# A second cross-attention's weights added up on VectorE alone, with side work split and moved by steps

## The chip, the cores and the metric

The kernel runs on one core of a Trainium2 chip, in float32 throughout. The time is the device time of one execution in microseconds (us); of several executions the median is taken.

## The reference, cut to what matters

Four layers are added to x one after another. The arrays are x [4, 512, 256] and the context ctx [4, 1601, 256].

```python
x = x + L0_xattn(ctx, layernorm(x))   # 8 heads of 128; keys and values of [ctx; latents]
x = x + L0_ffn(layernorm(x))          # 8 experts, top 2, each with a capacity; h = gelu(xb @ w1); y = h @ w2
x = x + L1_xattn(ctx, layernorm(x))   # 8 heads of 32
x = x + L1_ffn(layernorm(x))          # 8 experts, top 2, no capacity

def L1_xattn(key, query):             # key = value = ctx, 1601 rows; query has 512
    q, k, v = split_heads(query @ Wq.T), split_heads(key @ Wk.T), split_heads(key @ Wv.T)
    attn = softmax(einsum('bhnd,bhmd->bhnm', q, k) * 32 ** -0.5)
    return einsum('bhnm,bhmd->bhnd', attn, v)      # heads joined again
```

## The kernel before, in words

The program has four stages in a row, one for each layer.

**First attention.** It takes the four batches one after another, and beside the last ones it already routes rows to the experts of the next stage (`route`: `normalize`, `choose`, `send`). `send` scatters the rows `xn` of a batch into the array `slot_x` in DRAM, with eight indirect transfers on GpSimd's queue (L312).

**First FFN** (`all_experts`). Each of the 8 experts has 512 places, taken in two halves. For each expert `fetched` loads the rows `sx` from `slot_x` and two weight matrices through SyncE's queue; `turned` transposes the rows on TensorE, `hidden` does the first matrix (ps_h) and the GELU, and `results` the second (ps_y). A generator `beside` is advanced between these pieces. In half 0 it is `keys_first`, which routes and sends the last batch and projects keys and values of batch 0 (`keys_values`); in half 1 it is `keys_next`, which projects those of batch 1, gathers and adds the first FFN's results of batch 0 (`collect`, `add_collected`), makes its queries and the first maxima. Another generator, `clears`, is advanced four times an expert: it writes zeros into the second half of `slot_y` and then fills `rows_a` and `rows_b`, the arrays in DRAM into which the second FFN's rows will be scattered, with 41 transfers. Between the halves the program loads a register and branches on it (L1286), in case an expert has too many rows. The instructions of this stage are ordered by a scheduler, apart from the places with a manual order.

**Second attention.** Its 16 units are (batch b, head group o of four heads, half f of the 512 queries). A unit has 13 tiles j of 128 keys, the last with 65 rows. For each tile `weights` computes scores in transposed form: keys on partitions, four heads times 256 queries on the free axis, by four matmuls into one PSUM tile ps_w. The left operand `keyed` holds the keys of a head group and a row of ones, the right one `asked` the queries and, at rows 32 and 96, the negated maximum of each query, so that the exponential on ScalarE needs no further shift. That exponential gives `pT`. `weigh` multiplies it with the values, accumulating over the tiles in ps_o. `add_weights` adds the `pT` of all tiles element by element, into `sum0` on VectorE and `sum1` on GpSimd:

```python
by_pool = (1, 4, 7, 10)
...
(nc.gpsimd if k else nc.vector).tensor_tensor(to, to, pT[:r], ALU.add)
```

Tiles 0 and 1 are written straight into the two sums; so VectorE adds 8 tiles of a unit and GpSimd 3. `closing` reduces the sums over the partitions by matmuls with ones (ps_n), transposes (tp_o), divides, and adds to x. It runs in three pieces, two steps apart.

The maxima of a unit are computed a unit ahead: `maxima` has TensorE form the scores once more with queries on partitions (ps_s, 7 pieces a unit) and VectorE reduce each of them (`tops`, L1124), `negated` reduces over the pieces into `shift`, and `to_row` turns `shift` into the rows of `asked`, by four transposes (ps_r, L1146) and two copies on ScalarE (L1150). ps_w, ps_s and all side work share a PSUM pool of three tiles.

In this stage the four computing engines follow the order in which the program is written (`in_order`). The loop takes two tiles a step, 104 steps and a few to finish; a step number counts tiles. In each step come the `weights` of two tiles, a piece of `maxima`, then for the two tiles of the step before the adds, then `weigh`, and last what `put` has placed at this step: `negated`, `to_row`, the gathers of `collect`, `queries` of the next batch, `keys_values` of the batch after, and `route2` of the batch before, which is the routing of the second FFN and ends in the scatters of its rows (L539). Transfers on SyncE's queue keep no such order, but are issued one after another.

**Second FFN.** It works on tiles of 128 scattered rows, whose number per expert is a matter of the routing; `route2` of the last batch runs at its start, beside tiles that the other batches have already filled.

## Time and profile before

| | |
|---|---|
| median of three executions | 2905.28 us (2904.32 to 2910.24) |
| the profiled execution, its own time | 2910.62 us |
| its span on the core | 2908.8 us |
| its mean granted TensorE clock | 0.972 |
| first attention | 0 to 1575 us of the span |
| first FFN | 1575 to 1943 us |
| second attention | 1943 to 2617 us |
| second FFN | 2617 to 2909 us |

The profile names engines PE (TensorE's matmuls), PEld (its weight loads), DVE (VectorE), ACT (ScalarE), POOL (GpSimd) and SP (SyncE); a q behind the name marks the engine's queue of transfers. A group's line gives the line of the kernel, engine, operation, output and inputs, their shapes and the number of instructions, then busy us and mean ns of one, then the idle time ahead of them with what ended most of it. A line of the timeline gives start, duration, and the same names, with the idle time ahead in brackets. A line of waits gives what waited, for whom, the total us, how often and the longest. The stage borders above are read from the first matmul of each stage. A granted clock of 1.00 is full speed.

### The profile page before, as it was taken

The page shows a single profiled execution, that of the slowest core. Times are in us where ns is not written, and L with a number is a line of the kernel's source. Part 1 is how long each engine was busy: PE and PEld are TensorE (multiplying, and loading weights), DVE is VectorE, ACT ScalarE, POOL GpSimd, SP SyncE. Part 2 cuts the span into 40 slices and gives each one's busy share as a digit, 9 for nine tenths or more (in the row PEclk, how much of TensorE's full clock was granted, in tenths as well). Part 3 has the DMA queues.
Part 4 walks back from the last instruction along what each step waited for, and adds up shares of the span by engine and source line. Part 5 has one row for each costly group of instructions (what it writes and reads, how often), then busy time and mean ns, then how long its engine had stood idle before and what let it go on. Part 6 is the DMA issues. An engine that isn't in the chain of part 4 may idle for free. (4 is left out here: it accounts for less than half of the span.)

```text
span 2908.8 us, 36010 instructions
## 1 busy us (share of the span) xinstructions
PE 2746.4 (94%) x13614; PEld 1860.1 (64%) x13614; DVE 1460.5 (50%) x2339; ACT 935.3 (32%) x1325; POOL 379.8 (13%) x290
## 2 busy tenths in 40 slices
PE   6999999999999999999998799998989989799998
PEld 2666666766766667666666577864444454458887
DVE  6445556554476444554454302148876767763111
ACT  3323334332343223332332111124434434352221
POOL 0000000100001000000000101002223414152442
PEclk9999999999999999999999999999999999899999
DMA  5444343434344333333335698820001011106563
GB/s 164 111 113 114 97 110 92 109 93 99 89 111 107 97 89 93 97 92 102 95 97 150 197 241 238 236 72 23 23 12 61 24 38 35 39 31 223 161 214 99
DMA packets 196435, 311.96 MB, mean 107 GB/s; under 512 B 43319, under 2 KB 117368, under 8 KB 193560
## 3 DMA queue, kind: packets, MB, share of 16 engines
q1 hardware_dynamic: 157512, 227.52, 29.4%
q0 software_dynamic: 14160, 46.31, 5.4%
q10 hardware_dynamic: 24576, 35.68, 4.8%
q8 instruction: 112, 1.84, 0.3%
q14 instruction: 75, 0.61, 0.1%
HBM read 111.73 MB, written 51.34 MB: 56 GB/s over the span
## 5 line engine op out<-in xcount | busy, mean ns | idle before, releaser
L810 DVE TENSOR_REDUCE top<-ps_s 128x1 f32<-128x2113 f32 x128 | 301.8, 2358 | 581.7 <-PE ps_s L802 581.7
L839 PE MATMUL ps_o<-pT,v 128*128 128x256 f32 x2176 | 521.7, 381 | 0.5 <-DVE inv L817 0.5
L802 PE MATMUL ps_s<-kT,qT 128*128 128x512 f32 (+1 forms) x1280 | 489.0, 526 | 6.0 <-ACT attn L816 6.0
L839 PEld LDWEIGHTS ps_o<-pT,v 128*128 128x128 f32 x2176 | 410.0, 191 | 115.1 <-issue 68.4
L816 ACT ACTIVATE attn<-ps_s,top 128x2113 f32<-128x2113 f32 x128 | 259.0, 2024 | 476.4 <-DVE top L810 446.1
L802 PEld LDWEIGHTS ps_s<-kT,qT 128*128 128x128 f32 x1280 | 241.4, 190 | 252.8 <-issue 236.7
L831 DVE STREAM_TRANSPOSE pT<-swapped 128x2176 f32<-128x2176 f32 x128 | 312.4, 2441 | 33.6 <-DMA swapped<-attn 23.3
L1124 DVE TENSOR_REDUCE tops<-ps_s 128x2 f32<-128x1024 f32 (+1 forms) x224 | 238.0, 1105 | 152.0 <-PE ps_s L1113 151.6
L1387 PE MATMUL ps_w<-asked,keyed 64*128 64x256 f32 (+1 forms) x1664 | 247.4, 420 | 20.3 <-DVE tops L1124 9.5
L751 PE MATMUL ps_k<-kvin,wkv 128*128 128x512 f32 (+1 forms) x640 | 262.7, 533 | 3.3 <-DVE mv_g L689 1.7
L785 PE MATMUL ps_v<-wkv,kvin 128*128 128x256 f32 x1088 | 254.5, 381 | 1.4 <-ACT v L792 1.4
L1387 PEld LDWEIGHTS ps_w<-asked,keyed 64*128 64x128 f32 (+1 forms) x1664 | 149.0, 192 | 147.0 <-ACT pT L1400 61.6
L1400 ACT ACTIVATE pT<-ps_w 128x1024 f32<-128x1024 f32 (+1 forms) x176 | 179.5, 1024 | 195.2 <-PE ps_w L1387 191.8
L785 PEld LDWEIGHTS ps_v<-wkv,kvin 128*128 128x128 f32 x1088 | 204.8, 190 | 36.6 <-ACT v L792 5.9
L1409 DVE TENSOR_TENSOR sum<-sum,pT 128x1024 f32<-128x1024 f32 (+1 forms) x128 | 183.0, 1430 | 10.3 <-ACT pT L1400 4.0
L764 ACT ACTIVATE kT<-ps_k,bqk 128x512 f32<-128x512 f32 (+1 forms) x160 | 96.9, 620 | 266.1 <-PE ps_k L751 123.4
L1409 POOL TENSOR_TENSOR sum<-sum,pT 128x1024 f32<-128x1024 f32 x48 | 122.5, 2553 | 350.3 <-ACT pT L1400 350.1
L751 PEld LDWEIGHTS ps_k<-kvin,wkv 128*128 128x128 f32 x640 | 115.9, 191 | 77.3 <-issue 66.7
L1113 PE MATMUL ps_s<-kv,qT 32*128 32x512 f32 (+1 forms) x1024 | 135.9, 579 | 14.7 <-ACT kv L1017 6.5
L792 ACT COPY v<-ps_v 128x512 f32<-128x512 f32 x144 | 79.9, 561 | 216.7 <-PE ps_v L785 142.1
L1197 PE MATMUL ps_h<-sxT,w 128*128 128x256 f32 x512 | 118.6, 390 | 4.8 <-ACT hT L1204 4.1
L1211 PE MATMUL ps_y<-w,hT 128*128 128x256 f32 x512 | 114.5, 380 | 0.3 <-DVE y L1219 0.2
(300 smaller groups left out, 2662.8 us busy)
## 6 DMA issues: line engine op xcount, KB each, us to landing
swapped<-attn SPq DMA_DIRECT2D x1536, 68.0 KB, 2.0
swapped<-attn ACTq DMA_DIRECT2D x512, 68.0 KB, 2.2
w<-in_w_dram SPq DMA_DIRECT2D x32, 1024.0 KB, 6.2
rows_b<-empty SPq DMA_DIRECT2D x36, 530.0 KB, 14.3
w_e<-in_wall_dram SPq DMA_DIRECT2D x5, 2052.0 KB
cw<-in_ctxT_dram SPq DMA_DIRECT2D x4, 1601.0 KB, 6.4
keyed<-kv SPq DMA_DIRECT2D x32, 200.1 KB, 3.6
ctx_b<-in_ctx_dram SPq DMA_DIRECT2D x3, 1536.0 KB
```

What stands on the lines that cost most here:

```text
L751: nc.tensor.matmul(ps[:, :n], lhsT=wkv[:, c, hs], rhs=kvin[:, c, : NB - 1, k, :] if k < 4 else kvin[:, c, NB - 1, :, :], start=c == 0, sto ...
L785: nc.tensor.matmul(ps[:, k, :], lhsT=flat_kvin[c][:, j * P : (j + 1) * P], rhs=wkv[:, c, cols], start=c == 0, stop=c == DC - 1,)
L802: nc.tensor.matmul(flat[:, j0 : j0 + n], lhsT=qT[:, t * P : (t + 1) * P], rhs=kT[:, j0 : j0 + n], start=True, stop=True,)
L810: nc.vector.tensor_reduce(top, flat[:, :L], AX.X, ALU.max, negate=True)
L816: nc.scalar.activation(attn[:, :L], flat[:, :L], AF.Exp, bias=top, accum_out=total)
L831: nc.vector.transpose(pT[:, :, k * P : (k + 1) * P].rearrange("p c (a i) -> p a c i", a=4), swapped.rearrange("p a (c i) -> p a c i", i=32),)
L839: nc.tensor.matmul(ps, lhsT=v[:, j - parts[part][0], (h % 2) * DH0 : (h % 2 + 1) * DH0], rhs=pT[:, j, :], start=j == 0, stop=j == NB - 1,)
L1113: nc.tensor.matmul(pss[i // 2][:, i % 2, at : at + n], lhsT=qTs[b][rows, o, q0 : q0 + P], rhs=kvs[b][0][o][rows, j0 : j0 + n], start=True, ...
L1124: nc.vector.tensor_reduce(tops[u][:, t : t + at // n, 2 * pair : 2 * pair + 2, j0 // 512], of, AX.X, ALU.max,)
L1387: nc.tensor.matmul(ps[:r, s, pair * QH : (pair + 1) * QH], lhsT=keyed[o][64 * s : 64 * s + 64, pair, j * P : j * P + r], rhs=asked[u % 3][ ...
L1400: nc.scalar.activation(pT[:r], ps[:r], AF.Exp)
L1409: (nc.gpsimd if k else nc.vector).tensor_tensor(to, to, pT[:r], ALU.add)
```

## The change

- `add_weights` works on VectorE only: tile 0 starts the sum, tiles 1 to 11 are added to it, and the last tile, of 65 rows, is not added, but summed over its own rows by `closing`'s matmuls. `sum1` is gone, and the pool of `pT` has 8 tiles where it had 6.
- `shift` has a quarter of its size. `negated` is one reduction, `to_row` one transpose and four activations on ScalarE, which scale by a column of `in_row` to leave zero in the rows that are not meant. Both come earlier: at 7 and 5 tiles ahead of the unit, where it was 5 and 4.
- The pieces of `closing` come one step earlier. `weigh` is issued ahead of the adds, and where the last tile of a unit and the first of the next are weighed in one step, the first of the next is put off to the following step (`late`).
- `route2` and `queries` yield more often, and lists of steps (`beside`, `bare`) place the pieces: a consumer is put a step or more after its producer. The counts (`counted`) are copied out of PSUM, the copy of `wbT` goes to ScalarE, and scatters go two to a yield. The gathers of `collect` come some 28 tiles earlier, and their zeros are written by GpSimd; `add_collected` comes four tiles earlier.
- In the first FFN `send` of the last batch moves to the end of half 0. The 41 fills of `rows_a` and `rows_b` move to the second attention, one for each tile from step 2 on. The first `keyed` tile is prepared at the end of half 0, the second at step 4 of the second attention and loaded at step 8. Three pieces of the maxima of unit 1 and `to_row` of unit 0 move into half 1, and `beside` is advanced three times an expert.

The diff, cut to its core (the added yields and some moved copies are left out):

```diff
--- before.py
+++ after.py
...
@@ -327,7 +331,7 @@
...
             g = gat.tile([P, D], F32, tag="g", name="g")
-            nc.vector.memset(g, 0.0)
+            nc.gpsimd.memset(g, 0.0)
             nc.gpsimd.indirect_dma_start(
...
@@ -489,11 +510,18 @@
...
         )
-        if b == B - 2:
-            nc.vector.tensor_copy(taken_a, taken2)
+        counted = two.tile([P, n, E], F32, tag="counted", name="counted")
+        nc.vector.tensor_copy(counted, ps)
+        tp = psum.tile([P, 4, P], F32, tag=tag, name="tp_w")
+        for t in range(n):
+            nc.tensor.transpose(tp[:E, t, :], wb[:, t, :], ident)
+        wbT = two.tile([E, n * P], F32, tag="wbT", name="wbT")
+        nc.scalar.copy(wbT, tp[:E, :n].rearrange("p i q -> p (i q)"))
+        yield
         for k in range(2):
             off, place, at, out_of = small("off2"), wide("place"), small("at2"), small("out_of")
-            nc.vector.tensor_tensor(place, hot[k], ps, ALU.mult)
+            nc.vector.tensor_tensor(place, hot[k], counted, ALU.mult)
             nc.vector.tensor_reduce(off, place, AX.X, ALU.add)
...
@@ -512,13 +540,25 @@
...
                 nc.vector.memset(place_a[k][:, mine_b], int(NOWHERE))
-        yield
-        tp = psum.tile([P, 4, P], F32, tag=tag, name="tp_w")
-        for t in range(n):
-            nc.tensor.transpose(tp[:E, t, :], wb[:, t, :], ident)
-        wbT = two.tile([E, n * P], F32, tag="wbT", name="wbT")
-        nc.vector.tensor_copy(wbT, tp[:E, :n].rearrange("p i q -> p (i q)"))
+            yield
+        def scatters():
...
+        sending = scatters()
         for t0 in range(0, n, 2):
...
@@ -1049,19 +1085,50 @@
...
     asked = [soon.tile([P, 2, QH], F32, name=f"asked{i}") for i in range(3)]
-    shift = [soon.tile([P, 2, 2, P], F32, name=f"shift{i}") for i in range(2)]
+    shift = [soon.tile([P, P], F32, name=f"shift{i}") for i in range(2)]
     for t in shift + asked:
...
+    keyed = [soon.tile([P, 2, M], F32, name="keyed0")]
+    def load_keys(b, o):
+        for pair in range(2):
+            for s in range(2):
+                i = 2 * pair + s
+                nc.sync.dma_start(
+                    keyed[o][64 * s : 64 * s + 32, pair, :],
+                    kvs[b][0][o][i * DH1 : (i + 1) * DH1, :],
+                )
+    def init_keys(t):
+        of_ones = ones[:, 0:1].to_broadcast([P, M])
+        nc.scalar.activation(t[:, 0], of_ones, AF.Copy, scale=in_row[:, 0:1])
+        nc.vector.tensor_scalar(t[:, 1], of_ones, in_row[:, 1:2], None, ALU.mult)
+    empty = soon.tile([P, PAY], F32, name="empty")
+    nc.gpsimd.memset(empty, 0.0)
+    nc.gpsimd.memset(empty[:, D : D + 1], NOWHERE)
...
         xn = soon.tile([P, NT, D], F32, tag="xn", name="xn")
-        mv = ln_moments(turns, x[b], NT)
-        root = ln_root(turns, mv, NT)
+        mv = ln_moments(turns, x[b], NT, some=())
+        for i in range(NT):
+            ln_moments(turns, x[b], NT, mv=mv, some=(i,))
+            if i + 1 < NT:
+                yield
+        ve = ln_variance(turns, mv, NT)
+        yield
+        root = ln_root(turns, mv, NT, ve)
         yield
...
             ln_apply(xn, x[b], mv, rs, i)
-        yield
+            if i in (0, NT - 1):
+                yield
         xnT = soon.tile([P, DC, S], F32, tag="xnT", name="xnT")
...
@@ -1129,25 +1197,26 @@
...
     def negated(u):
-        for pair in range(2):
-            nc.vector.tensor_reduce(
-                shift[u % 2][:, :, pair, 32::64],
-                tops[u][:, :, 2 * pair : 2 * pair + 2, :],
-                AX.X,
-                ALU.max,
-                negate=True,
-            )
+        nc.vector.tensor_reduce(
+            shift[u % 2].rearrange("q (s c) -> q s c", s=2)[:, :, 32:36],
+            tops[u].rearrange("q t (p s) n -> q s (t p) n", s=2),
+            AX.X,
+            ALU.max,
+            negate=True,
+        )
         tops.pop(u)
     def to_row(u):
-        ps = banks["m"].tile([P, 2, QH], F32, tag="m", name="ps_r")
-        for pair in range(2):
+        ps = banks["m"].tile([P, P], F32, tag="m", name="ps_r")
+        nc.tensor.transpose(ps, shift[u % 2], ident)
+        for r in (32, 96):
             for t in range(2):
-                nc.tensor.transpose(
-                    ps[:, pair, t * P : (t + 1) * P], shift[u % 2][:, t, pair, :], ident
-                )
-        for r in (32, 96):
-            nc.scalar.copy(asked[u % 3][r : r + 1], ps[r : r + 1])
+                nc.scalar.activation(
+                    asked[u % 3][r : r + 4, :, t * P : (t + 1) * P],
+                    ps[r : r + 4].unsqueeze(1).to_broadcast([4, 2, P]),
+                    AF.Copy,
+                    scale=in_row[r : r + 4, 2 + t : 3 + t],
+                )
...
@@ -1237,36 +1307,32 @@
...
-        empty = rt.tile([P, PAY], F32, name="empty")
-        nc.gpsimd.memset(empty, 0.0)
-        nc.gpsimd.memset(empty[:, D : D + 1], NOWHERE)
-        def clears():
...
-        clear = clears()
-        kvs = []
+        def clear_results(e):
+            tc.keep_in_program_order(
+                nc.sync.dma_start(
+                    slots(slot_y, e, 1), empty[:, :D].unsqueeze(1).to_broadcast([P, CT, D])
+                )
+            )
...
             choose()
-            send()
             yield
...
             kvs.append(kv)
-            for k, f in enumerate(steps):
+            for f in steps:
                 f()
-                if k % 2:
-                    yield
+                yield
+            for _ in range(len(steps) + 2, 3 * E - 4):
+                yield
+            send()
+            init_keys(keyed[0])
+            yield
+            load_keys(0, 0)
...
@@ -1311,10 +1375,13 @@
...
             negated(0)
-            to_row(0)
+            for g in range(3):
+                maxima(1, g)
+                yield
+                if g == 0:
+                    to_row(0)
         all_experts(1, keys_next())
-        assert next(clear, None) is None
...
@@ -1350,31 +1417,15 @@
...
         two = st.enter_context(tc.tile_pool(name="c_two", bufs=2))
-        six = st.enter_context(tc.tile_pool(name="c_six", bufs=6))
+        some = st.enter_context(tc.tile_pool(name="c_some", bufs=8))
         ps_s = st.enter_context(tc.tile_pool(name="c_ps_s", bufs=3, space=PSUM))
...
-        keyed = [one.tile([P, 2, M], F32, name=f"keyed{o}") for o in range(DC)]
-        of_ones = ones[:, 0:1].to_broadcast([P, M])
-        for t in keyed:
-            nc.scalar.activation(t[:, 0], of_ones, AF.Copy, scale=in_row[:, 0:1])
-            nc.vector.tensor_scalar(t[:, 1], of_ones, in_row[:, 0:1], None, ALU.mult)
-        def load_keys(b, o):
...
-        by_pool = (1, 4, 7, 10)
+        keyed.append(one.tile([P, 2, M], F32, name="keyed1"))
...
@@ -1391,22 +1442,18 @@
...
                     )
-            k = int(j in by_pool)
-            if j in (0, by_pool[0]):
-                pT = two.tile([P, 2, 512], F32, tag=f"sum{k}", name=f"sum{k}")
-                sums[u, k] = pT
+            if j == 0:
+                pT = two.tile([P, 2, 512], F32, tag="sum", name="sum")
             else:
-                pT = six.tile([P, 2, 512], F32, tag="pT", name="pT")
+                pT = some.tile([P, 2, 512], F32, tag="pT", name="pT")
+            if j in (0, NM - 1):
+                sums[u, int(j > 0)] = pT
             nc.scalar.activation(pT[:r], ps[:r], AF.Exp)
...
         def add_weights(u, j, pT):
-            k = int(j in by_pool)
-            if j in (0, by_pool[0]):
-                return
-            r = rows_of(j, NM, TAIL)
-            to = sums[u, k][:r]
-            (nc.gpsimd if k else nc.vector).tensor_tensor(to, to, pT[:r], ALU.add)
+            if 0 < j < NM - 1:
+                nc.vector.tensor_tensor(sums[u, 0], sums[u, 0], pT, ALU.add)
...
@@ -1436,8 +1483,8 @@
...
                         ps[i * DH1 : (i + 1) * DH1, :],
-                        lhsT=ones[:, :DH1],
-                        rhs=sums[u, k][:, s, pair * QH : (pair + 1) * QH],
+                        lhsT=ones[: (P, TAIL)[k], :DH1],
+                        rhs=sums[u, k][: (P, TAIL)[k], s, pair * QH : (pair + 1) * QH],
                         start=k == 0,
...
@@ -1524,31 +1571,44 @@
...
+        ends = []
+        def place(step, gen, offsets):
+            for k in offsets:
+                put(step + k, lambda: next(gen, None))
+            ends.append(gen)
         for u in range(1, n_units):
-            put(NM * u - 5, lambda u=u: negated(u))
-            put(NM * u - 4, lambda u=u: to_row(u))
+            put(NM * u - 7, lambda u=u: negated(u))
+            put(NM * u - 5, lambda u=u: to_row(u))
             put(NM * u - 12, lambda u=u: load_queries(u))
...
                 put(s0, lambda b=b: load_keys(b, 1))
-                spread(s0 + 10, route2(b - 1, one, ps_s, "s"), 2, 24)
+                beside = (4, 8, 10, 18, 20, 22, 24, 28, 30, 32, 34, 36, 38, 40, 42, 44, 46)
+                bare = (4, 8, 10, 12, 12, 14, 14, 16, 18, 20, 22, 24, 26, 28, 30, 32, 34)
+                steps = beside if b + 1 < B else bare
+                place(s0, route2(b - 1, one, ps_s, "s"), (*steps, *range(steps[-1] + 2, 54, 2), *range(54, 62)))
             if b + 1 < B:
...
                 for k, f in enumerate(steps):
-                    put(s0 + 1 + k, f)
+                    put(max(s0 - 28, 0) + 1 + k, f)
                 for t in range(NT):
                     put(
-                        s0 + 14 + 2 * t,
+                        s0 + 10 + 2 * t,
                         lambda b=b, got=got, t=t: add_collected(b + 1, got, (t,)),
...
-                spread(s0 + 22, later(), 2, 5)
+                place(s0, later(), range(12, 32, 2))
             if 1 <= b and b + 1 < B:
...
@@ -1566,13 +1626,12 @@
...
-        load_keys(0, 0)
-        load_keys(0, 1)
+        for k, f in enumerate(clear_rows()):
+            put(2 + k, f)
+        put(4, lambda: init_keys(keyed[1]))
+        put(8, lambda: load_keys(0, 1))
         ordered = st.enter_context(in_order(*computing))
-        for g in range(3):
-            maxima(1, g)
         ahead = {}
...
@@ -1591,22 +1651,29 @@
...
                         maxima(*g)
-            for h in held:
-                add_weights(*h)
-            for uw, jw, pT in held:
+            late, todo = [], late + held
+            for uw, jw, pT in todo:
+                if jw == 0 and held and held[0][:2] == (uw - 1, NM - 1):
+                    late = [(uw, jw, pT)]
+                    continue
                 if jw == 0:
...
                     next(ending)
-                    put(step + 4, lambda ending=ending: next(ending))
-                    put(step + 6, lambda ending=ending: next(ending, None))
+                    put(step + 2, lambda ending=ending: next(ending))
+                    put(step + 4, lambda ending=ending: next(ending, None))
+            for h in held:
+                add_weights(*h)
             for k in range(step, step + 2):
...
         assert not at and not ahead, (sorted(at), sorted(ahead))
+        assert all(next(gen, None) is None and gen.gi_frame is None for gen in ends)
...
```

## The prediction

> **What bounds the kernel now.** I read the page's head and slices first, then busy time by stage, the waits of TensorE in the stage that the change names, and the timeline around its longest waits.
>
> ```profile
> span 2908.8 us, 36010 instructions
> PE 2746.4 (94%) x13614; PEld 1860.1 (64%) x13614; DVE 1460.5 (50%) x2339; ACT 935.3 (32%) x1325; POOL 379.8 (13%) x290
> ```
>
> TensorE (PE) is the bound of the whole, so time can come only from its idle time and from stretches at a low clock. Stages by window (first attention, first FFN, second attention, second FFN; the last columns are granted clock, DMA share, GB/s):
>
> ```profile
> 0.00:1575.00 1575.00, 1543.11 (x5725) 1038.22 (x5726) 815.21 (x1122) 515.84 (x715) 46.81 (x69) 1.00 0.41 105
> 1575.00:1943.00 368.00, 329.10 (x1478) 263.48 (x1476) 90.96 (x183) 65.00 (x101) 18.98 (x20) 0.93 0.74 204
> 1943.00:2617.00 674.00, 600.60 (x5050) 318.33 (x5048) 496.07 (x758) 285.82 (x343) 209.63 (x120) 0.94 0.11 32
> 2617.00:2909.00 292.00, 273.56 (x1366) 240.09 (x1366) 58.30 (x278) 68.69 (x167) 104.39 (x81) 0.98 0.56 174
> ```
>
> The first 1575 us keep their order: nothing to gain. The first FFN has 39 us of PE idle, the second attention 73, both at a clock of 0.93 to 0.94. What ended the idle in the second attention (total, times, longest):
>
> ```profile
> PE ps_r L1146 <- DVE shift L1133: 17.0, 6, 4.4
> PE ps_w L1387 <- DVE tops L1124: 9.5, 5, 4.6
> PE ps_b L526 <- DVE wbT L521: 8.6, 3, 2.9
> PE ps_o L1418 <- ACT oT L1430: 7.0, 8, 0.9
> PE ps_s L1113 <- ACT kv L1017: 6.5, 2, 3.3
> PE ps_c L486 <- DVE earlier L482: 6.1, 3, 2.8
> ```
>
> All are VectorE (DVE) arriving late, or ScalarE behind it. The timeline of one such place shows why:
>
> ```profile
> 2039.18 2.55 DVE L1409 TENSOR_TENSOR sum<-sum,pT 128x1024 f32<-128x1024 f32 x2
> ...
> 2045.34 2.36 DVE L1124 TENSOR_REDUCE tops<-ps_s 128x2 f32<-128x1024 f32 x2 [0.90 <-PE ps_s L1113]
> 2047.61 3.40 DVE L1409 TENSOR_TENSOR sum<-sum,pT 128x1024 f32<-128x1024 f32 x1
> ```
> ```profile
> 2047.58 2.35 POOL L1409 TENSOR_TENSOR sum<-sum,pT 128x1024 f32<-128x1024 f32 x1 [8.27 <-ACT pT L1400]
> ```
> ```profile
> 2055.58 0.66 PE L1146 MATMUL ps_r<-ident,shift 128*128 128x128 f32 x4 [3.23 <-DVE shift L1133]
> ```
>
> An add alone is 1.22 us; beside GpSimd's (POOL) add it took 3.40, and 8 us later PE waits 3.23 us for `shift`. Of the 128 adds 27 are stretched, each beside a POOL add: mean 1430 ns against 1220, 27 us in all. In the first FFN one wait stands out:
>
> ```profile
> 1678.41 1.12 PE L1187 MATMUL tp_x<-ident,sx 128*128 128x128 f32 x4 [20.39 <-DMA sx<-slot_x]
> 1680.31 6.13 PE L1197 MATMUL ps_h<-sxT,w 128*128 128x256 f32 x16 [0.78 <-DVE sxT L1188]
> ```
>
> `sx` is read back from slot_x after the last batch's eight row scatters on POOL, each waiting for the landing of the one before:
>
> ```profile
> 1650.28 0.99 POOL L312 DMA_INDIRECT slot_x<-xn,slot  x1 [10.43 <-DMA slot_x<-xn,slot]
> ...
> 1673.33 0.98 POOL L312 DMA_INDIRECT slot_x<-xn,slot  x1 [1.55 <-DMA slot_x<-xn,slot]
> ```
>
> **The change, part by part, against the profiled run's 2910.6 us** (it stands 5.3 us above the median of 2905.3).
>
> *First FFN.* The eight scatters move to the end of half 0, so half 0 no longer waits for them: −20.4 us. The 16 matmuls after that wait took 6.13 us; the same 16 with no idle ahead take 3.6 (the next group): −2.5. The scatters need not be done before half 1: eight at the uncrowded 2.6 us each are 21 us, and they may start when the last expert's `sx` has landed, whose load is now issued at 1712 where half 0 ends at 1773: about 58 us of PE work cover them; the crowded ones at 9 to 11 us each (1639 to 1659) would make about 80, 22 too many. The 41 fills of rows_a and rows_b, which crowd them now, leave this stage, so I take 21 us: hidden. Behind them on POOL stand the gathers of collect(0), which half 1 uses only after six pieces of keys. At the stage's end maxima of unit 1 and the first to_row move into FFN work: idle of 1.26 and 2.75 us there goes, with some half clock (12 matmuls 4.34 us against 3.5): −5, and −2 for initial copies into `keyed`. Moving LayerNorm side work may remove a 3.77 us wait for hT at 1795: 0 to −5, I take 0. Sum −30; range −37 to −5 (the low end if the scatters are crowded).
>
> *Second attention.* Its 674 us are about 549 of PE work at full clock (instruction counts times undisturbed durations: a key tile's four ps_w matmuls 1.07, weigh 0.5, a maxima piece 1.13, closing 1.65), 73 idle, 46 lost at half clock (14 half-clock records, 92 us), and 6 of small gaps. After:
> 1. to_row is one transpose for four: 16 x 3 x 0.17 = −8 on PE, +1 elsewhere: work 541.
> 2. VectorE. A unit needs 12 long reduces x 1.14, two short x 0.35, adds, 1.0 for its closing, 0.1 shift. Adds rise from 8 to 11 and are 1.14 (first of a step) or 1.34 (second, on the same accumulator): 13.6, so 29.0 a unit, where PE's unit is 13.9 + 6.5 + 7.5 + 1.8 = 29.7. With side work (55 us of DVE, 66 of PE) VectorE has 519 of work, PE 541. The 27 us of stretching go with the POOL adds. So VectorE is nearly the second bound: a plain step of two key tiles costs it 2.27 + 2.48 = 4.75 us, PE 4.33; the steps with one add or none pay back. I walked the 104 steps in the new order, carrying DVE's excess and letting PE wait when it passes 0.75 us (three PSUM banks give 2.1 us between a maxima and the reuse of its bank, less one reduce and the handover 0.2): PE waits 42 us in 39 steps, the longest 2.3. A slack of 0.3 gives 48, one of 2.0 gives 30. The same walk on the old order gives 26, with waits at the places of the 3.9 us (2017) and 4.6 us (2503) idle; its other 47 come from stretched adds, `shift` in the next step, oT, and the routing's waits (ps_b, ps_c). The change gives each of these one more step or an earlier one.
> 3. Waits for pT, kv, the first cw and oddments: 16 in the trace, 10 kept.
> 4. Clock: the 92 us at half clock followed idles of 2.78 to 4.62 us, of which the stage has 14 (46 us in all); its 32 idles of 0.3 to 1.13 us lowered nothing, and there is none between. The longest now walked, 2.3, lie in that gap: I keep 5 us (range 0 to 30).
> 5. ScalarE: four small activations where two copies were (578 ns each), 16 x 2 x 0.58 = 19 us more on an engine 42% busy, and each row of `asked` 1.2 us later; to_row moves one step earlier (4.9 us), which covers it; if not, 16 x 1.2 = 19. GpSimd loses 122 us of adds and takes the memsets of 24 gathers from VectorE (272 ns there, no row for GpSimd; between 0.3 and the 2.4 of its larger add, I take 1): a batch ahead, so hidden. If each stretched a DVE add by up to 2.2 us, 53; by their share of time, 24 of 610 us, 2.
> 6. SP's queue gets the 41 fills, two in each of the first 21 steps of two tiles: 21 MB in some 100 us, 210 GB/s where 241 is the most in any slice, and four of them held SP 6.35 us at 1645. Behind them in SP's queue stand load_queries and the keys of the second half (issued at tile 8, needed at 26, 40 us on; key loads take 3.6 us now); POOL's gathers share the transfers. Two fills of 14 us ahead fit in the 40: 0 to +10, I take 2.
>
> 541 + 42 + 10 + 5 + 2 + 2 + 6 of small gaps = 608: −66 (range −90 to −30).
>
> *Second FFN.* Routing of the last batch finishes later and its square root is exposed for about 2 us; gathers come 10 us later, with 34 us between landing and use now (2685, used 2724): +1 (−4 to +5).
>
> Sum −30 − 66 + 1 = −95: 2815.6 in the profiled execution, 2810.3 with its 5.3 taken off. I say 2812.
>
> [...] Row first: the waits of `ps_r` and `ps_w` above, up to 4.4 and 4.6 us, cost the clock, the 0.3 to 1.13 us ones did not; 39 short waits should leave it full. [...] I follow the row, because 32 short idles in this stage left the clock full[...].
>
> **Rivals.**
> - *VectorE's waits are longer than walked (0.17).* Adds at 1.34 throughout and ScalarE's pT late would bring 16 x 11 x 0.1 = 18 us, and with slack near 0 another 8, plus the clock at 15 more: the stage gains 25, all −55: 2850. For: VectorE at 519 of 607. Against: reduces at 1.136 to 1.14 in undisturbed pairs are steady.
> - *Late scatters (0.08).* If they stay at 10 us each, 80 us pass, 22 beyond the last expert; the branch at L1286 holds every engine (it costs 2.96 now). The first FFN gains 5: 2837.
> - *The clock gate, slower than before (0.08).* Half-clock time costs half of itself. All other gains are 95 + 5, so from about 200 us of half clock in the second attention, where 92 are now, the change loses; at 230 it ends near 2923. Against it: no idle under 2.75 us did it in this stage or just before it.
> - *It does not do what it says (0.04).* Stretching needs only some POOL work: memsets and gathers also run there. Indirect DMAs beside adds show no stretch now; with half the 27 us left and the routing waits as they were: 2835.
>
> **How the numbers follow.** My forecast 0.63 at 2812 (2785 to 2835 by its own bounds: first FFN ±8, VectorE's slack ±12, clock +15). Range 2770 to 2860: it takes in 2837, 2850 and the low ends together (−37, −90), and leaves out the clock case and deeper gains. A measurement of this kernel can tell about 0.2%, 6 us. Faster 0.89, same 0.03, slower 0.08.
>
> **What would show it.** Right: no add over 1.4 us at the stage, no `shift` wait, waits of ps_s or ps_w for tops some 40 us in total with none above 2.5, a clock of 0.98 or more in the second attention, which lasts about 608; no 20 us wait for sx, the first FFN near 338. Wrong: a clock below 0.9 in the second attention, tops waits above 60 us, or idle ahead of the branch.

## The result, and the profile after

The changed kernel took 2854.72 us (median of five runs, 2852.68 to 2859.92), the one before 2905.28 (2901.82 to 2913.05): a ratio of 0.9824, 95% interval 0.9806 to 0.9841. Measured again in a later comparison the ratio was 0.9823 (0.9804 to 0.9843). The gain is about 51 us where 93 had been forecast: inside the range, a little over half of the size.

The head of the page of the changed kernel, and its group of adds (busy us, mean ns):

```profile
span 2851.0 us, 35962 instructions
...
PE 2710.0 (95%) x13566; PEld 1844.4 (65%) x13566; DVE 1468.9 (52%) x2343; ACT 946.7 (33%) x1362; POOL 255.8 (9%) x271
...
L1456 DVE TENSOR_TENSOR sum<-sum,pT 128x1024 f32<-128x1024 f32 x176 | 214.8, 1220 | 12.3 <-PE ps_o L1465 3.6
```

176 adds stand where 128 were, at a mean of 1220 ns where it was 1430. GpSimd has 124 us less of work. The stages by window, as before:

```profile
0.00:1578.00 1578.00, 1542.33 (x5729) 1037.99 (x5729) 820.10 (x1130) 517.99 (x717) 46.08 (x64) 1.00 0.41 105
1578.00:1924.00 346.00, 325.10 (x1469) 261.42 (x1468) 83.71 (x171) 61.65 (x100) 21.56 (x31) 0.96 0.62 182
1924.00:2541.60 617.60, 566.92 (x5003) 302.15 (x5003) 508.23 (x771) 295.82 (x375) 81.65 (x93) 0.98 0.20 53
2541.60:2851.00 309.40, 275.60 (x1366) 242.83 (x1366) 56.81 (x272) 71.22 (x170) 106.56 (x83) 0.95 0.54 165
```

To compare like with like I take the borders at the same events in both traces: the first `tp_x`, the first `ps_w`, the end of the last `ps_f` or `tp_o`. Idle is the sum of gaps over 0.25 us between TensorE's matmuls; the price of the clock is half of the time at half clock that was not idle (in the trace of before a 128x256 matmul of `ps_h` starts 216 ns after the last one at full clock, 427 at half); the rest is work at full clock with small gaps.

| stage | before | after | difference | of it idle | clock | work | forecast |
|---|---|---|---|---|---|---|---|
| first attention | 1579.7 | 1577.9 | −1.8 | | | | 0 |
| first FFN | 363.3 | 346.2 | −17.1 | −13.5 | −3.6 | 0.0 | −30 |
| second attention | 673.7 | 617.5 | −56.2 | −21.2 | −29.7 | −5.3 | −66 |
| second FFN | 292.2 | 309.4 | +17.2 | +14.8 | +3.9 | −1.4 | +1 |

So the second attention did nearly what was forecast, and its largest term is the clock, not the idle time. Most of the rest of the forecast was lost at two borders, where the trace has two waits that the trace before did not have.

**Border one: the fills did not wait for the second attention.** The timeline of SyncE's queue in half 1 of the first FFN, then TensorE:

```profile
1871.92 22.07 SPq L395 DMA_DIRECT2D rows_b<-empty  x10
1894.10 3.12 SPq L1248 DMA_DIRECT2D w<-in_w_dram  x1
```
```profile
1910.54 9.94 PE L1280 MATMUL ps_y<-w,hT 128*128 128x256 f32 x32 [8.19 <-DMA w<-in_w_dram]
```

Ten fills held the queue for 22 us ahead of the last expert's second weights. TensorE waited 8.19 us for these, and the 32 matmuls after the wait took 9.94 us where the same 32 take 7.07 elsewhere: 11 us. `put` places an instruction in the program; the four computing engines keep that order in the second attention, SyncE does not, and nothing that a fill reads was late.

**Border two: the scatters of batch 2 now end after the second attention.** GpSimd, VectorE and ScalarE in the timeline at the border, then TensorE:

```profile
2545.70 0.98 POOL L550 DMA_INDIRECT rows_b<-pay,place_b  x1 [1.84 <-DMA rows_b<-pay,place_b]
...
2548.98 0.75 DVE L127 BATCH_NORM_STATS2 st<-x 128x6 f32<-128x256 f32 x2 [9.55 <-DMA rows_b<-pay,place_b]
...
2551.17 1.28 ACT L144 ACT_TABLE_LOAD   x1 [10.44 <-DMA rows<-rows_a]
...
2552.46 0.20 ACT L144 ACTIVATE rs<-ve 128x4 f32<-128x4 f32 x1
2552.69 1.28 ACT L1408 ACT_TABLE_LOAD   x1
...
2553.98 0.84 ACT L1408 ACTIVATE cw<-ps_f,w_kv 128x256 f32<-128x256 f32 x2
```
```profile
2537.88 3.70 PE L1400 MATMUL ps_f<-cw,w_g 128*128 128x256 f32 x16
2554.87 1.12 PE L1391 MATMUL tp<-ident,cw 128*128 128x128 f32 x4 [13.29 <-ACT cw L1408]
```

Read from the bottom: TensorE waits for a GELU (`cw`), which stands on ScalarE behind the square root of the last routing (`rs`), which waits for VectorE's moments (`st`), which wait until the last scatter has landed near 2549. (For the square root the profile names the load of `rows`, but VectorE ends its part, `ve`, at 2551.0, just ahead of it.) The moments do not use what is scattered; by the trace their first write waits for the landing of `rows_b<-pay`. That it does so because the second FFN's tiles take memory that the second attention used is a reading, not shown.

The sixteen scatters run one after another, 2.9 us apart on average. The first and the last of batch 2, in the kernel before and in the changed one (there the last is shown above):

```profile
2553.14 0.99 POOL L539 DMA_INDIRECT rows_a<-pay,place_a  x1 [0.16 <-issue]
...
2614.29 0.98 POOL L539 DMA_INDIRECT rows_b<-pay,place_b  x1 [3.24 <-DMA rows_b<-pay,place_b]
```
```profile
2502.52 0.98 POOL L550 DMA_INDIRECT rows_a<-pay,place_a  x1 [64.58 <-DVE out_of L532]
```

Before, the first starts 64 us ahead of the end of its stage (2616.7), the last one lands about as the stage ends, and the last GELUs stand ahead of the square root. After the change the first starts only 39 us ahead of the end (2541.6), and the chain takes 46. The shorter stage explains little of this: shortened by a twelfth, the 64 us would be 58 (an estimate). The larger part is the new place of the routing. The first scatter was placed at tile 24 of the batch, and the places that it needs were computed at tile 18; the longer list of steps computes them at tile 32, and a tile takes some 3 us.

Within the second attention, what ended TensorE's idle time (total, times, longest):

```profile
PE ps_w L1438 <- ACT pT L1451: 19.7, 22, 2.5
PE ps_w L1438 <- DVE tops L1192: 11.0, 8, 1.9
PE ps_s L1181 <- ACT pT L1451: 4.1, 7, 1.0
PE ps_w L1438 <- issue: 3.6, 2, 2.5
PE tp L173 <- DVE tops L1192: 2.2, 4, 0.9
PE ps_b L566 <- DVE tops L1192: 2.1, 2, 1.0
```

`shift`, `oT`, `wbT` and `earlier` are gone. VectorE is behind about 20 us of waits in all, ScalarE's exponentials behind 25.

### The profile page after: what moved, and what is told of

It reads as the page before. It is cut to its first block, busy times and chain, and to the rows that moved or that the text cites. A ratio compares the mean times of both kernels' runs of the same rounds, so it can differ in the third digit from the quotient of the medians.

```text
span 2851.0 us, 35962 instructions
## 1 busy us (share of the span) xinstructions
PE 2710.0 (95%) x13566; PEld 1844.4 (65%) x13566; DVE 1468.9 (52%) x2343; ACT 946.7 (33%) x1362; POOL 255.8 (9%) x271
## 5 line engine op out<-in xcount | busy, mean ns | idle before, releaser
L1438 PE MATMUL ps_w<-asked,keyed 64*128 64x256 f32 (+1 forms) x1664 | 237.8, 407 | 39.4 <-ACT pT L1451 19.7
L1451 ACT ACTIVATE pT<-ps_w 128x1024 f32<-128x1024 f32 x192 | 195.6, 1024 | 219.4 <-PE ps_w L1438 211.9
L1456 DVE TENSOR_TENSOR sum<-sum,pT 128x1024 f32<-128x1024 f32 x176 | 214.8, 1220 | 12.3 <-PE ps_o L1465 3.6
L1280 PEld LDWEIGHTS ps_y<-w,hT 128*128 128x128 f32 x512 | 99.2, 196 | 26.9 <-issue 13.1
```

Of the source, the lines that this page charges most:

```text
L1280: nc.tensor.matmul(ps[:, t, :], lhsT=hT[:, f, t * P : (t + 1) * P], rhs=w2[:, f, :], start=f == 0, stop=f == FC - 1,)
L1438: nc.tensor.matmul(ps[:r, s, pair * QH : (pair + 1) * QH], lhsT=keyed[o][64 * s : 64 * s + 64, pair, j * P : j * P + r], rhs=asked[u % 3][ ...
L1451: nc.scalar.activation(pT[:r], ps[:r], AF.Exp)
L1456: nc.vector.tensor_tensor(sums[u, 0], sums[u, 0], pT, ALU.add)
```

## The experiments

Twelve runs, each of five rounds beside the kernel before on one chip. Ratios are to the kernel before, with their 95% intervals; the changed kernel stands at 0.9824.

### The two borders

**fills_later.**

```diff
+        fill = one.tile([P, PAY], F32, name="fill")
+        def start_fills():
+            nc.gpsimd.memset(fill, 0.0)
+            nc.gpsimd.memset(fill[:, D : D + 1], NOWHERE)
+        put(2, start_fills)
-        for k, f in enumerate(clear_rows()):
+        for k, f in enumerate(clear_rows(fill)):
```

> The changed kernel with one edit: the 41 fills of rows_a and rows_b read a tile that GpSimd writes only at step 2 of the second attention, so SyncE cannot issue them in the first FFN. In the changed kernel 19 of them went out from 1842 us on, and the last expert's second weights were issued at 1894 behind ten of them; TensorE waited 8.2 us for those weights and ran the next 32 matmuls in 9.94 us for 7.07. Theory (fills cost the missing part of the first FFN): the wait and its half clock go, 11 us less, 2844 us; the second attention within 3 us of 617. Rival (the fills only change place, and delay the keys and queries that stand behind them on SyncE's queue): the first FFN gains 11 and the second attention loses as much, 2855 us.

2849.5 us, 0.9786 (0.9767 to 0.9805). The windows of the first FFN and the second attention:

```profile
1581.00:1920.00 339.00, 326.56 (x1469) 261.82 (x1469) 83.84 (x171) 61.89 (x102) 21.61 (x31) 0.96 0.48 154
1920.00:2538.50 618.50, 569.67 (x5003) 302.75 (x5003) 508.84 (x772) 295.87 (x375) 81.83 (x95) 0.98 0.30 71
```

The wait for the weights is gone, the first FFN is 7 us shorter and the second attention within 1 us, at 71 GB/s for 53. The ratio's step of 0.004 is 11 us. The theory holds, though this trace shows 7 of its 11 us in the first FFN; the rival does not.

**before_fills** puts the same edit into the kernel before (with `filling = clear_rows(fill)` and one `next(filling, None)` for each tile from step 2 on).

> The kernel before with the 41 fills held back until step 2 of the second attention, and send where it was, ahead of the first FFN's half 0. Theory (the fills crowd the eight scatters, and the scatters' own latency of 2.6 us is the rest): the scatters run at 2.6 to 3 us each, done near 1661 where it was 1674; the 20.4 us wait for sx falls to 5 to 9; the program 10 to 14 us shorter. Rival (the wait is set by when the scatters can start, not by the fills): the wait stays at 17 to 20 us.

2895.2 us, 0.9966 (0.9953 to 0.9978), 10 us less. The scatters end at 1663 where it was 1674, and of the wait that the change takes away by moving `send` more than half goes by the fills alone:

```profile
PE tp_x L1187 <- DMA sx<-slot_x: 8.2, 1, 8.2
```

**sqrt_last.**

```diff
+            with ExitStack() as first_of:
+                if i == 0:
+                    first_of.enter_context(in_order(nc.scalar))
                 for _ in range(3):
                     next(rest, None)
```

> The changed kernel with one edit: the square root of the last batch's routing is held behind the last GELU of the second attention on ScalarE (in the changed kernel it stood ahead of the last two GELUs, and waited for the scatters of batch 2 to land). Theory (order on ScalarE turns late scatters into a wait of TensorE): the 13.3 us wait at the stage border falls to 2 to 5 us, since TensorE has 7 us of ps_y and 7 of ps_h that need no scatter; 8 to 11 us less, 2845 us. Rival (the wait is for memory or PSUM that the second attention holds until the scatters have read their rows): the wait stays above 10 us, 2855.

2857.4 us, 0.9818 (0.9799 to 0.9837): no more than 2 us by the ratio, 3 by the window of the second FFN (306.1). The wait moved:

```profile
PE ps_h L1400 <- DVE xT L1392: 9.5, 1, 9.5
```

VectorE too has the moments ahead of the first turned rows. The order on ScalarE is one of two queues in which the scatters' lateness is passed on, so this edit alone settles little. The theory did not have that second queue; the rival's wait of more than 10 us is there (0.9 for `cw` and 9.5 here), and its cause, memory held for the scatters, was not shown.

**no_rows_b.**

```diff
             for rows, at in ((rows_a, place_a), (rows_b, place_b))[b == B - 1 :]:
+                if b == B - 2 and rows is rows_b:
+                    continue
```

> The changed kernel without the eight scatters of batch 2 into rows_b (the second FFN's further tiles then lack these rows; all instructions on TensorE, VectorE and ScalarE stay). Theory (the scatters of batch 2 end 7 us after the second attention): the last scatter lands near 2527 in place of 2548, the 13.3 us wait falls below 3 us, and its half clock of 3 goes, 13 to 16 us less: 2840 us. Rival (the wait comes from the order on ScalarE and the table loads alone): 2 to 4 us less.

2852.8 us, 0.9800 (0.9782 to 0.9818): 7 us less than the changed kernel by the ratios, whose intervals overlap, so the reading rests on the trace. The wait at the border:

```profile
PE tp L1393 <- ACT cw L1410: 4.0, 1, 4.0
```

13.3 us fell to 4.0, and the second FFN from 309.4 to 300.3; the moments now start at once. The scatters' end is the cause of 9 of the 13 us; the 4 that stay are, as an estimate from the timeline of the changed kernel above, the square root, its two table loads and the GELUs behind them (0.20, twice 1.28 and 0.84: 3.6 us), a part that the theory had put at "below 3". (The first FFN was 6 us longer in this trace, with 13.1 us for the last weights: the fills, again.)

**fills_and_scatters**, with the edit of fills_later and these:

```diff
-                bare = (4, 8, 10, 12, 12, 14, 14, 16, 18, 20, 22, 24, 26, 28, 30, 32, 34)
+                bare = (4, 6, 8, 10, 10, 12, 12, 14, 16, 18, 20, 22, 24, 26, 28, 30, 32)
...
-            for rows, at in ((rows_a, place_a), (rows_b, place_b))[b == B - 1 :]:
-                for k in range(2):
+            for k in range(2):
+                for rows, at in ((rows_a, place_a), (rows_b, place_b))[b == B - 1 :]:
...
                 nc.vector.memset(place_a[k][:, mine_b], int(NOWHERE))
+            next(sending)
             yield
```

> The changed kernel with two edits: the fills held back as in fills_later, and the routing of a batch sends its rows earlier: the last one's pieces begin up to 2 tiles earlier, and the scatters of the first choice start as soon as its places are known, ahead of the second choice and of the bias, so 6 to 8 tiles earlier (15 to 20 us). Theory (the late scatters of batch 2 make the 13.3 us wait): they land 5 to 12 us before the second attention ends, the wait falls below 2 us, and with the 8 to 11 us of the first FFN the program is 20 to 26 us shorter than the changed kernel, ratio to before near 0.975. Rival (the order on ScalarE, with the square root ahead of GELUs, makes the wait by its table loads, as some of it stayed with fewer scatters): 4 us of the wait stay, ratio 0.977; and more work early in the last batch adds waits for VectorE.

2843.1 us, 0.9789 (0.9769 to 0.9809). The second attention and the second FFN:

```profile
1914.00:2543.60 629.60, 572.53 (x5003) 304.13 (x5001) 510.37 (x783) 295.39 (x375) 88.96 (x97) 0.97 0.28 71
2543.60:2840.30 296.70, 275.29 (x1366) 242.31 (x1366) 54.60 (x262) 71.08 (x170) 104.45 (x81) 0.97 0.54 169
```

The first scatter starts at 2493.0, 51 us ahead of the stage's end where it was 39, and the last is issued at 2535.9. The border wait fell to 4.1 us (the theory said below 2, the rival 4) and the second FFN by 12.7, but 12.5 came back in the second attention, as the rival feared: 6.6 of idle (4.5 for the first rows, `cw<-rows_a`, since the scatters into rows_a now end later, and 9 more of waits for `tops`, less some others) and 5.7 of clock.

**scatters_sooner** has of these edits only the added `next(sending)` (and the fills), with the old order of the scatters and the old steps; **scatters_sooner_sqrt_last** adds the edit of sqrt_last.

> The changed kernel with the fills held back as in fills_later and the scatters of a batch started 4 tiles sooner, two with each choice's places, in their old order (rows_a first) and with the pieces of routing at their old steps. Theory (in fills_and_scatters the second attention lost 7 us of new idle to the earlier pieces and to the later end of rows_a's scatters, 4.5 us of it at the first rows' load): the second attention back at 617 to 621, the wait at the stage border 13.3 down to 3 to 6 us; ratio to before 0.974 to 0.977. Rival (that loss lay in GpSimd and in the clock's windows, not in those two): the second attention stays near 630, ratio 0.979.

> As scatters_sooner, and the square root of the last routing held behind the last GELU as in sqrt_last. Theory (with the scatters landed, what is left of the border wait is the square root and its two table loads ahead of the last GELUs): 2 to 4 us less than scatters_sooner. Rival (VectorE's order, its moments ahead of the turned rows, keeps the rest): the same as scatters_sooner within 1 us.

2844.4 us, 0.9789 (0.9770 to 0.9807), and 2840.1 us, 0.9779 (0.9761 to 0.9797). The second attention is back at 617.6, but the border wait is 12.3 us: the edit did nothing. The first scatter in scatters_sooner:

```profile
2492.84 0.98 POOL L527 DMA_INDIRECT rows_a<-pay,place_a  x1 [63.38 <-DVE out_of L549]
```

It stands 39.1 us ahead of the end of its stage (2531.9), as in the changed kernel: GpSimd had nothing else to do and already began as soon as VectorE had the first places. Only an earlier routing brings the scatters forward. What scatters_sooner gains, it gains by the fills. The last kernel has the lowest median here, 13 us below the changed kernel by the ratios, whose intervals do not overlap, but only 2 below fills_later, within the noise; its border wait is 7.6 us, on VectorE.

### The second attention

**pool_adds.**

```diff
+        by_pool = (1, 4, 7, 10)
...
-            if 0 < j < NM - 1:
-                nc.vector.tensor_tensor(sums[u, 0], sums[u, 0], pT, ALU.add)
+            k = int(j in by_pool)
+            if j in (0, by_pool[0]):
+                return
+            r = rows_of(j, NM, TAIL)
+            to = sums[u, k][:r]
+            (nc.gpsimd if k else nc.vector).tensor_tensor(to, to, pT[:r], ALU.add)
```

> The changed kernel with the adds of the weights as before: tiles 4, 7 and 10 of a unit on GpSimd into a second sum, the last tile added on VectorE, 6 buffers for pT; all else as changed. Theory (adds beside GpSimd's were stretched, and side work spread by steps has made less of it matter): about 27 us of stretching return on VectorE, which has 50 us less of adds, and some waits for shift with them; the second attention 5 to 15 us longer, 2860 to 2870 us. Rival A (VectorE is the second bound now, so fewer adds there shorten it): 5 to 10 us less. Rival B (the stretched adds were the main cost): 25 us longer, 2880.

2873.3 us, 0.9870 (0.9851 to 0.9889). Second attention:

```profile
1927.00:2571.20 644.20, 578.37 (x5003) 307.10 (x4999) 489.06 (x739) 295.60 (x376) 212.42 (x143) 0.95 0.21 52
```
```profile
PE ps_w L1439 <- ACT pT L1452: 27.1, 21, 9.4
...
PE ps_n L1489 <- POOL sum L1461: 11.5, 1, 11.5
```

27 us longer, by rival B's size (15 of it idle, 12 clock), but not by its mechanism alone. 20 adds are stretched, 20 us of VectorE's time, and waits for `tops` are no worse, 8.0 us. The new long waits are for GpSimd's adds, which stand in GpSimd's order among the scatters and come late (one holds a `pT` buffer that the next exponential needs, of which this kernel has 6 where the changed one has 8; one holds up the sum that `closing` needs). The scatter and the add behind the 9.4 us wait:

```profile
2440.63 1.66 POOL L550 DMA_INDIRECT rows_b<-pay,place_b  x1 [1.41 <-DMA rows_b<-pay,place_b]
2442.30 2.36 POOL L1461 TENSOR_TENSOR sum<-sum,pT 128x1024 f32<-128x1024 f32 x1
```

No wait for `shift` came back. The whole is only some 13 us slower than the changed kernel by the ratios, since with a longer stage the scatters end in time and the second FFN takes 300.2.

**adds_only** and **adds_weigh_first** put the headline alone into the kernel before (the edit of pool_adds the other way round); the second also has:

```diff
-            for h in held:
-                add_weights(*h)
             for uw, jw, pT in held:
...
+            for h in held:
+                add_weights(*h)
```

> The kernel before with the headline part alone: weights added on VectorE, the 65-row tile summed by its own matmul, 8 buffers for pT; side work, closing, to_row, fills and scatters as before. Theory (stretched adds are the larger part of the gain in the second attention, the spread of side work the smaller): no add over 1.3 us, the waits of ps_r for shift (17 us) mostly gone, but side work still in lumps, so waits for tops rise from 9.5 to about 25; the second attention 20 to 30 us shorter, 645 to 655. Rival (the adds pay only with the spread side work; alone VectorE's 50 us more of adds fall on the same lumps): within 8 us of 674.

> The kernel before with the headline part alone as in adds_only, and with weigh issued ahead of the adds. In adds_only the first tile's weigh read the running sum after the second tile's add (so its numbers, but not its amount of work, differ from the reference), and TensorE waited 19.0 us for those adds. Theory (the headline needs the other parts: with side work in lumps, VectorE's 50 us more of adds come back as waits for shift, tops and the routing, though no add is stretched): the 19 us go, the second attention falls from 715 to 680 to 690, still 5 to 15 longer than before's 674; 2912 to 2922 us. Rival (the loss of adds_only was that one wait and the clock after it; without it the stretched adds' 27 us are gained): the second attention 645 to 660, 2880 to 2890 us.

2942.9 us, 1.0133 (1.0110 to 1.0156), and 2915.5 us, 1.0039 (1.0024 to 1.0055). Of the second one, group, window and waits in the second attention:

```profile
L1404 DVE TENSOR_TENSOR sum<-sum,pT 128x1024 f32<-128x1024 f32 x176 | 214.7, 1220 | 14.6 <-PE ps_o L1413 5.1 <-ACT pT L1399 0.5 <-DVE sum L1404 0.5
```
```profile
1942.00:2619.10 677.10, 597.89 (x5050) 316.55 (x5048) 518.20 (x804) 285.31 (x343) 75.31 (x72) 0.94 0.11 32
```
```profile
PE ps_r L1146 <- DVE shift L1133: 19.4, 8, 3.7
PE ps_w L1386 <- DVE tops L1124: 10.5, 6, 4.8
PE ps_c L486 <- DVE earlier L482: 10.2, 3, 4.1
PE ps_b L526 <- DVE wbT L521: 7.4, 3, 2.7
```

No add is stretched any more, and the waits are those of the kernel before, a little longer: 677 us where it was 674, and 11 us more for the program by the ratio. So the theory holds, though it had put the stage 3 us longer still, and the headline alone is worth nothing. The other parts without it (pool_adds) take the stage from 674 to 644, and it takes 27 us more on top of them, to 617. For adds_only, with a stage of 715 us, both texts miss: its adds stand ahead of `weigh`, so the first tile's `weigh` waits for the second tile's add, and that cost 19 us of waits and 19 of clock besides.

**row_split.**

```diff
-            put(NM * u - 5, lambda u=u: to_row(u))
+            put(NM * u - 5, lambda u=u: to_row(u, (0,)))
+            put(NM * u - 3, lambda u=u: to_row(u, (1,)))
```

> The changed kernel with one edit: to_row's four activations are split, two at 5 tiles ahead of the unit, two at 3. In the changed kernel the four take 1.67 us in a row on ScalarE ahead of a tile's exponential, and TensorE then waits for a PSUM tile (22 waits, 19.7 us). Theory (to_row on ScalarE makes these waits): the waits of ps_w for pT fall from 19.7 to 8 to 12 us, the second attention 8 to 12 us shorter, about 607. Rival (the waits come from the table loads of the square roots and from the keys' copies on ScalarE, or VectorE takes their place): 0 to 3 us.

2863.2 us, 0.9850 (0.9830 to 0.9870). This misses on both sides:

```profile
1923.00:2553.00 630.00, 583.36 (x5003) 307.22 (x5003) 508.95 (x771) 299.29 (x375) 83.60 (x93) 0.96 0.20 52
```
```profile
PE ps_w L1443 <- ACT pT L1456: 15.2, 15, 2.6
PE ps_w L1443 <- DVE tops L1192: 13.6, 13, 2.2
```

The waits for `pT` fell by a quarter, idle time by 5 us in all, and the stage grew by 12.6: time at half clock rose from 20.5 to 54.6 us. Why waits so alike did that stays open in part; the count of the clock's windows at the end says where to look.

**changed_again** is the changed kernel beside these.

> The changed kernel itself, beside the three others on one chip. Theory: a ratio to before within 0.2% of 0.9824, about 51 us less.

2855.1 us, 0.9823 (0.9804 to 0.9843), with the same stages: 616 us for the second attention, 14.2 us at the border to the second FFN, 5.5 us for the last weights.

## Why the prediction was right, and where it was not

The time lies inside the range, but not within the forecast's own bounds of 2785 to 2835. That the range held is in part luck: its room was meant for other failures, and the two waits that took most of the shortfall are not among them. Between the two profiled executions 58 us were gained where 95 were forecast; of the 37 missing, 13 are lost in the first FFN, 10 in the second attention, 16 in the second FFN, and 2 came back in the first attention.

- **Second attention, −66 forecast, −56.2 measured.** The sum came near for other reasons than its terms. Work −8: −5.3. Idle, 73 to 54: by the count used here 67.7 to 46.5. VectorE's 42 us of waits were 20, below what the walk gives for any slack tried (30 at 2.0 us). The walk's handover of 0.2 us is more than the trace of before has: a reduce starts 0.02 to 0.05 us after the `ps_s` it waited for, and `ps_w` 0.05 us after the reduce it waited for. ScalarE, put at 10 us kept, was 25. The clock's 41 us of gain were 29.7, and this is the step that failed here. The prediction halved all of the 92 us at half clock, though part of it was idle and already counted as such, and 5 us of it lie ahead of the stage; by the count above 39.4 us were to be had, not 46. And 9.7 were still lost where 5 were kept, in 20.5 us at half clock.
- **ScalarE, item 5.** It was argued that `to_row` a step earlier covers its longer activations. It covers the unit that waits for the row, not the exponential that stands behind them on ScalarE. The worst place, where a square root's two table loads of 1.28 us (the first at 2129.91) come in the same step:

```profile
2131.20 0.21 ACT L144 ACTIVATE rs<-ve 128x4 f32<-128x4 f32 x1
2131.79 0.59 ACT L1069 COPY kv<-ps_v 128x512 f32<-128x512 f32 x1 [0.38 <-PE ps_v L1062]
2132.40 1.67 ACT L1214 ACTIVATE asked<-ps_r,in_row 4x256 f32<-4x256 f32 x4
2134.08 1.28 ACT L1451 ACT_TABLE_LOAD   x1
2135.38 1.02 ACT L1451 ACTIVATE pT<-ps_w 128x1024 f32<-128x1024 f32 x1
```
```profile
2136.45 1.14 PE L1438 MATMUL ps_w<-asked,keyed 64*128 64x256 f32 x8 [2.46 <-ACT pT L1451]
```

- **The reading of the stretched adds.** The prediction showed a stretched add, and 8 us later a wait for `shift`, and took the one for the cause. adds_weigh_first has no stretched add and 19.4 us of waits for `shift`, 17.0 before; pool_adds has 20 stretched adds and no such wait. So the other parts removed them: `negated` and `to_row` stand earlier and further apart, and the lumps of side work are spread. Which of these did it was not tried. The stretching was real, 27 us of VectorE's time; how much of it TensorE paid for no run separates, since the adds that replace GpSimd's give VectorE 22 us more to do in adds_weigh_first (518 us in the stage for 496).
- **First FFN, −30 forecast, −17.1 measured.** The 20.4 us wait went, its half clock and the idle at the end as well. The step that failed is "the 41 fills leave this stage": 20 went out in half 1 all the same and cost 11 us by the timeline (7 by the stage of fills_later). A further 2.5 us are the wait at the first `ps_w`. The rival of late scatters did not come: the eight were issued from 1682 to 1713, over before the branch near 1743, though 4.4 us apart where 2.6 was taken.
- **Second FFN, +1 forecast, +17.2 measured.** The term named the square root and gave it 2 us; it missed what the square root waits for. The step that failed is that only the last batch's routing was taken to finish later: that of batch 2 does too, so its scatters end 7 us behind the stage where they ended with it. no_rows_b and fills_and_scatters show it from two sides; the routing at its old steps was not tried. Gathers 28 us later (not 10) doubled a second wait, 3.5 to 7.0 us.
- **The clock.** The stage has some 50 waits where 39 were walked, more of them for ScalarE than for VectorE, at a granted clock of 0.98, so the conclusion held. But the reason given, that no short idle lowers the clock, is false: in the changed kernel, with waits of 1.08 and 1.11 us close together (the second to 1964.61) half clock began at 1963.99, and with 0.52 and 1.32 us (to 2421.20) at 2421.38. The reading of before was not whole either: of its 92 us at half clock 13.7, from 2521.5 on, follow no idle of more than 0.25 us in the window ahead.
- **The nearest rival, 2850, had the time and not the mechanism**: it took VectorE's waits to be longer than walked, and they were half.

## What to carry to other kernels

An edit that shortens a stage, or places its side work later, is to be followed to that stage's end: ask which serial chain there (here sixteen scatters, 46 us) now starts too late, and which engine's queue passes its lateness on. A place in the program binds only the engines that keep program order: here 20 fills placed in the second attention, which begins at 1924 us, went out from 1842 us on. To hold a transfer back, give it something late to read: in fills_later that shortened the first FFN by 7 us. Value a part of a change with the other parts in and with them out: here one part was worth +3 us of its stage alone and −27 us on top of the rest (+11 and −13 for the program, by the ratios).

## What the runs showed of the hardware

In the clock records of the 14 traces the start of every stretch of the granted clock lies on a grid of 3.413 us, within 0.005 us, and every stretch at half clock, but for those that the end of a trace cuts off, is a multiple of it. I counted TensorE's idle time (all gaps between matmuls) in each window of that grid from 1600 us to the last matmul:

| idle in a window | at full clock: windows, next one at half | at half clock: windows, next one still at half |
|---|---|---|
| none | 2993, 4 | 175, 21 |
| some, under 0.5 us | 1035, 2 | 55, 21 |
| 0.5 to 1.0 | 413, 17 | 42, 40 |
| 1.0 to 1.5 | 150, 6 | 18, 18 |
| 1.5 to 2.0 | 88, 50 | 5, 5 |
| 2.0 and more | 111, 111 | 58, 58 |

In these traces half clock went with the idle time of the window before: at full clock it followed all 111 windows with 2.0 us and more, 50 of 88 with 1.5 to 2.0, and 29 of 4591 with less. The length of a single wait does not tell it. The same wait of 2.46 us stands twice in the changed kernel's second attention. The one shown above, ending at 2136.45, is split by the grid into 0.67 and 1.79 us, and full speed stayed; the one ending at 2305.74 has 2.04 us in one window, and the next window was at half clock. Once at half clock, 121 of 123 windows with over 0.5 us of idle were followed by half clock again, where at full clock 184 of 762 such windows were followed by it. This fits row_split, whose waits for `ps_b` of 1.64 and 1.66 us were each followed by 13.7 us at half clock; that those small gaps were the cause was not tried. Idle time is not all of it: the six falls with under 0.5 us of idle all come behind a window with small matmuls of the routing (`ps_l`, 128x8, or `ps_b`, of 8 rows); why is open.

VectorE's add of two 128x1024 tiles took 1.22 us alone and up to 3.66 beside GpSimd's add of the same size; 27 took over 1.3 us in the kernel before and 20 in pool_adds. In the changed kernel, with no add on GpSimd, none of 176 passed 1.23 us, though 39 of them overlap one of GpSimd's indirect transfers; in adds_weigh_first the mean of 176 was 1220 ns. In all 86 places where the two adds overlap (46 in the kernel before, 40 in pool_adds) the one that ends second ended nearly its whole length alone (1.22 and 2.35 us) behind the other: VectorE's 1.08 to 1.14 us behind GpSimd's, or GpSimd's 2.20 to 2.25 us behind VectorE's. GpSimd's adds were longer there too, up to 3.41 us in the kernel before. What in the chip makes it so was not shown.
